# Two-layer graph attention: the second layer in steps of four key tiles, with logits in three pairs of banks and the mask applied in SBUF

## The chip, the cores and the metric

The kernel runs on one core of a Trainium2 chip. The metric is the device time of one execution in microseconds (us); of several runs the median is given. A profile shows one such execution. Engines are called PE or TensorE (matmuls), DVE or VectorE, ACT or ScalarE, POOL or GpSimd, and SP, whose queue issues the DMAs.

## The reference

Two attention layers over a graph of 4096 nodes with 512 features, 8 heads of 64, each with layer norm and a residual.

```python
# layer 0 (additive attention); adj holds edge weights, about 0 or up to 1e9
h = relu(layernorm(x))
d = (h @ W.T + b).reshape(N, 8, 64)
e = leaky_relu(src(d)[h, n] + trg(d)[h, m], 0.01) + adj
x = x + softmax(e, over m) @ d
# layer 1 (dot-product attention, masked)
h = relu(layernorm(x))
q, k, v = h @ Wq[head], h @ Wk[head], h @ Wv[head]
a = q @ k.T / 8 - 1e16 * (1 - max(adj, eye))
x = x + concat(softmax(a, over keys) @ v) @ Wo
```

All in float32.

## The kernel before

The program works through three stages. A preparation makes the first layer's values and logit parts and goes through the rows of `adj` in sets. The first layer runs over 8 query blocks of 512 queries by 32 key tiles of 128 keys; in the same loop it turns the rest of `adj` into a byte mask for the second layer, written to DRAM as `m_d`. It ends each query block by `finish` (normalise, residual, layer norm) and `project`, a generator whose matmuls are taken up in small portions by `fill(n)`, and which writes keys, queries and values of the second layer to `k_d`, `q_d`, `v_d`. `step_endings()` moves every unfinished generator of `endings` one `yield` on. The order of all instructions is the order in which the Python program issues them (a manual schedule); each engine works through its own queue in that order and waits for semaphores where data or buffers need it.

The change is in the second layer. Its work is 8 query blocks x 4 head pairs = 32 rounds, counted by `j`; a round has 32 key tiles of 128 keys, for two heads and 512 queries. Before, a step `s` covers two key tiles, so a round has `ST` = 16 steps and there are 512 steps. A step issues:

- `scores(s)` (L684): for each of two tiles four matmuls of 64x64x512, for the two heads and two halves of the tile, into a pair of PSUM banks, tag `q0` or `q1` (a pair holds 128x1024 f32: keys on partitions, heads and queries along the row).
- `exps` (L690): ScalarE's exponential of each tile, in place in PSUM.
- `masked` (L698): VectorE multiplies the exponentials in PSUM by the byte mask `mk` in SBUF and writes the product to `ring`, a buffer of 16 rows of 512 that holds 8 tiles (`share(t)`).
- `paired` (L703): GpSimd adds the two tiles of the step into `adds` (in a round's first step into `sums`).
- `gained(s - 1)` (L708): VectorE adds the last step's `adds` to `sums`, which becomes the denominators.
- `attended(s - 2)` (L716): four matmuls of values by `ring`, accumulated into `ot` over a round, in bank `m0` or `m1`.
- `fill` (project or output matmuls, L442) and `step_endings`.

The matmuls of `attended` lag two steps behind the logits, so that exponentials and masks of a step have time while TensorE works on others. At a round's end `divide(j)` copies `ot` to `both`, sums `sums` over partitions by a matmul with ones (`sp`, L730), sends the result through DRAM (`dd_d`, L734; `den`, L737) into a layout in which VectorE can take reciprocals (`rc`, L740), sends these through DRAM again (`rb`, L745) and lets GpSimd scale the output (L747). After four rounds `output` (L442, L759) applies `Wo`. Keys, values and queries of the next round (`load_keys`, `load_values`, `load_queries`) and masks of the next block (`load_mask`, two buffers of 2 MB) are loaded ahead by SP.

PSUM has eight banks: `q0` and `q1` (two each), `m0`, `m1`, `m2`, `s`. In the first layer `m0` and `m1` also serve `values` and `project`; in the second `project` uses `m1` and `m2`.

Of the kernel before, what the change touches and what calls it, by code (L numbers as in the profile page):

```python
# [8 lines left out]
F32 = mybir.dt.float32  # L9
I32 = mybir.dt.int32  # L10
U8 = mybir.dt.uint8
AF = mybir.ActivationFunctionType
# [5 lines left out]
P = 128  # L18
# [12 lines left out]
def tile_fast(  # L31
# [69 lines left out]
    q_d = dram.tile([NK, HC, P, W], F32, name="q_d")  # L101
    k_d = dram.tile([HC, P, N], F32, name="k_d")
    v_d = dram.tile([HC, P, NT, P], F32, name="v_d")
    dd_d = dram.tile([NK, HC, 2, W], F32, name="dd_d")
    rd_d = dram.tile([NK, HC, 2, W], F32, name="rd_d")

    def rows_of(t, n):
# [8 lines left out]
            nc.sync.dma_start(rows_of(t, n)[a], of[bass.ts(a, SQ)])  # L116

    ring = big.tile([P, 16, W], F32, name="ring")
    l0 = ExitStack()
    ppen = l0.enter_context(tc.tile_pool(name="pen", bufs=2))  # L120
    pmu = l0.enter_context(tc.tile_pool(name="mu", bufs=2))
# [127 lines left out]
    def prepare(pre):  # L249
# [113 lines left out]
            nc.scalar.activation(th[:, tiles], t, AF.Exp, scale=SLOPE - 1.0)  # L363

        def values(g, n, tiles):
            vp = ps.tile([P, tiles, W], F32, tag=("m0", "m1", "q1")[n], name="vp")
            for i in range(tiles):
                for kc in range(KC):
                    nc.tensor.matmul(
                        vp[:, i], lhsT=hT2[:, g % 2, kc, bass.ts(n + i, P)], rhs=wt[:, kc],  # L370
                        start=(kc == 0), stop=(kc == KC - 1),
                    )
            return vp
# [72 lines left out]
            if next(e, e) is e:  # L446
                endings.remove(e)

    banks = ["m0", "m1"]
    weights = {}  # L450

    def project(k, h1T):

        at = [0]

        def bank():
            at[0] += 1
            return ps.tile([P, W], F32, tag=banks[at[0] % 2], name="mp")

        def across(w, c, to):  # L460
            mp = bank()
# [174 lines left out]
    l0.close()  # L636


    ST = NT // 2
    ppa = ctx.enter_context(tc.tile_pool(name="pa", bufs=1))  # L640
    pq = ctx.enter_context(tc.tile_pool(name="q", bufs=3))
    prb = ctx.enter_context(tc.tile_pool(name="rb", bufs=2))
    pss = ctx.enter_context(tc.tile_pool(name="ss", bufs=1))
    total = NK * HC * ST
    banks[:] = ["m1", "m2"]
    ks, vs, qs, ms_, oTs, scs = {}, {}, {}, {}, {}, {}
    adds = ppa.tile([P, 2, 2, W], F32, name="adds")
    sums = ppa.tile([P, 2, 2, W], F32, name="sums")
    b6 = big.tile([P, AR * QK], F32, tag="B6", name="b6")
    wot = b6[:, N:].rearrange("p (c o) -> p c o", c=HC)  # L650

    def load_keys(j, cols):
        if j < NK * HC:
# [15 lines left out]
            qs[j] = pq.tile([P, W], F32, name="qt")  # L669
            nc.sync.dma_start(qs[j], q_d[j // HC, j % HC])  # L670

    def load_mask(k):
        if k < NK:
            ms_[k] = big.tile([P, NH * W], I32, tag=("B2", "B4")[k % 2], name="mk")
            nc.sync.dma_start(ms_[k], m_d[k])

    def scores(s):
        j, n = divmod(s, ST)
        for i in range(2):
            sc = scs[2 * s + i] = ps.tile([P, 2, W], F32, tag=f"q{i}", name="sc")  # L680
            for half in range(2):
                for h in range(2):
                    rows = bass.ts(h, D)
                    nc.tensor.matmul(  # L684
                        sc[bass.ts(half, D), h], lhsT=ks[j][rows, bass.ds((2 * n + i) * P + half * D, D)],
                        rhs=qs[j][rows], start=True, stop=True,
                    )

    def exps(t):
        nc.scalar.activation(scs[t], scs[t], AF.Exp, bias=shift, scale=1.0 / D**0.5)  # L690

    def share(t):
        return ring[:, bass.ts(t % 8, 2)]

    def masked(t):
        n = t % NT
        m = ms_[t // (HC * NT)].bitcast(U8).rearrange("p (h i l) -> p h l i", h=NH, l=4)[:, n // 4, n % 4]
        nc.vector.tensor_tensor(share(t), scs.pop(t), m.unsqueeze(1).to_broadcast([P, 2, W]), ALU.mult)  # L698

    def paired(s):  # L700
        j, n = divmod(s, ST)
        to = sums[:, j % 2] if n == 0 else adds[:, s % 2]
        nc.gpsimd.tensor_add(to, share(2 * s), share(2 * s + 1))  # L703

    def gained(s):
        j, n = divmod(s, ST)
        if n > 0:
            nc.vector.tensor_add(sums[:, j % 2], sums[:, j % 2], adds[:, s % 2])  # L708

    def attended(s):  # L710
        j, n = divmod(s, ST)
        if n == 0:
            oTs[j] = ps.tile([P, W], F32, tag=f"m{j % 2}", name="ot")
        for i in range(2):
            for h in range(2):
                nc.tensor.matmul(  # L716
                    oTs[j][bass.ts(h, D)], lhsT=vs[j][:, 2 * n + i, bass.ts(h, D)],
                    rhs=share(2 * s + i)[:, h],
                    start=(n == 0 and i == 0), stop=(n == ST - 1 and i == 1),
                )  # L720

    def divide(j):
# [2 lines left out]
        to = outs[k][:, c]  # L725
        nc.scalar.copy(to, oTs.pop(j))
        yield
        sp = ps.tile([P, W], F32, tag="s", name="sp")
        for h in range(2):
            nc.tensor.matmul(sp[bass.ts(h, SQ)], lhsT=ones, rhs=sums[:, j % 2, h], start=True, stop=True)  # L730
        sS = pss.tile([P, W], F32, name="sS")
        nc.scalar.copy(sS[:D], sp[:D])
        for h in range(2):
            nc.sync.dma_start(dd_d[k, c, h : h + 1], sS[h * SQ : h * SQ + 1])  # L734
        yield
        d = den[:, j]
        nc.sync.dma_start(d, dd_d[k, c].rearrange("h (p i) -> p h i", i=4))  # L737
        yield
        rc = small.tile([P, 2, 4], F32, name="rc")
        nc.vector.reciprocal(rc, d)  # L740
        nc.sync.dma_start(rd_d[k, c].rearrange("h (p i) -> p h i", i=4), rc)
# [22 lines left out]
    with tc.manual_schedule():  # L764
        load_queries(0)
        early = (NK - 1) * W
        load_keys(0, slice(0, early))
        load_mask(0)
        load_values(0, slice(0, early // P))
        for s in range(total + 4):  # L770
            j, n = divmod(s, ST)
            if s == 13:
                load_keys(0, slice(early, N))
                load_values(0, slice(early // P, NT))
                load_queries(1)
                nc.sync.dma_start(wot, wo.rearrange("h d o -> (h d) o").rearrange("(c p) o -> p c o", p=P))
            if s == 15:
                load_keys(1, slice(0, N))
                load_values(1, slice(0, NT))
            if n == 2 and j > 0:  # L780
                load_keys(j + 1, slice(0, N))
            if n == 4 and j > 0:
                load_values(j + 1, slice(0, NT))
            if n == 8 and j > 0:
                load_queries(j + 1)
            if j % HC == 1 and n == 6:
                load_mask(j // HC + 1)
            if s < total:
                scores(s)
                for i in range(2):  # L790
                    exps(2 * s + i)
                for i in range(2):
                    masked(2 * s + i)
                paired(s)
            if 0 <= s - 1 < total:
                gained(s - 1)
            a = s - 2
            if 0 <= a < total:
                attended(a)
                if a == ST - 1:  # L800
                    both = big.tile([P, 2, KC, W], F32, tag="B3", name="both")
                    for i in range(NK):
                        outs[i] = both[:, i % 2]
            fill(4 if s < ST + 6 else 2 if n % 8 == 5 else 0)
            step_endings()
            if s < ST - 4:
                step_endings()
            if 0 <= a < total and a % ST == ST - 1:
                e = divide(a // ST)
                next(e)  # L810
                endings.append(e)
# [28 lines left out]
        tp = ps.tile([P, W], F32, tag="m1", name="okt")  # L840
        nc.tensor.transpose(tp[:1, :P], ok, ident)
        nc.vector.tensor_reduce(flag, tp[:1, :P], AX.X, ALU.min)

# [239 lines left out]
```

## Time and profile before

| | |
|---|---|
| runs | 4362.02, 4365.09, 4366.08 us; median 4365.09 us |
| the profiled execution, own time | 4363.34 us |
| its span, first to last instruction | 4361.5 us |
| mean granted TensorE clock | 0.983 |
| PE busy | 4147.6 us (95%) |
| DVE busy | 3767.8 us (86%) |
| ACT busy | 1577.6 us (36%) |
| POOL busy | 2118.4 us (49%) |
| DMA | 555.53 MB, mean 127 GB/s |

The second layer begins at about 2170 us and ends with the program. Busy time counts an instruction from its start to its end, also while it stands still for something. In the profile, `x480: 1212/1215/2120` behind a line means 480 instructions that took at least 1212, in the median 1215 and at most 2120 ns. In a timeline the first column is the start in us from the span's begin and the second the length, of one instruction or of a row of equal ones (`x2`); a bracket tells how long the engine had been idle and what it had waited for. Fp32 matmuls appear twice each in the counts.

### The profile page before, as it was taken

The numbers are of one execution on the slowest core, as the hardware profiler recorded it, in microseconds if no ns is written. First come the engines' busy times: TensorE is split into PE (matmuls) and PEld (weight loads), VectorE is DVE, ScalarE is ACT, GpSimd is POOL, SyncE is SP. The second block draws the span as 40 slices with busy tenths as digits, with TensorE's granted clock in tenths as the row PEclk, the third lists the DMA queues.
The fourth block names the chain that finished last, engine by engine and source line by source line (L and its number), as shares of the span: only waits on it lengthen the run. The fifth ranks groups of instructions, "written<-read, shape, count | busy, mean of one in ns | idle before, by whom it ended". The sixth has DMA issues, their size and how long they took to land.

```text
span 4361.5 us, 63046 instructions
## 1 busy us (share of the span) xinstructions
PE 4147.6 (95%) x23806; PEld 1133.3 (26%) x23806; DVE 3767.8 (86%) x4508; ACT 1577.6 (36%) x1830; POOL 2118.4 (49%) x1004
## 2 busy tenths in 40 slices
PE   6899899999989899999999999999999999999997
PEld 3422222222222222222222222222222222222222
DVE  5599999999999999977657888888888888888885
ACT  3311222222222222210135555555555555555553
POOL 3211212122221212203057888788778777788784
PEclk8999999999999999999999999999999999999999
DMA  7776566565566656543313222222213223222211
GB/s 196 223 191 181 172 169 181 161 195 166 164 178 180 188 154 181 157 125 90 133 59 142 77 84 95 87 83 93 107 65 110 88 68 107 88 89 86 88 59 33
DMA packets 384568, 555.53 MB, mean 127 GB/s; under 512 B 62016, under 2 KB 242496, under 8 KB 375040
## 3 DMA queue, kind: packets, MB, share of 16 engines
q1 hardware_dynamic: 384256, 551.42, 41.2%
q8 instruction: 189, 3.10, 0.3%
q14 instruction: 123, 1.01, 0.1%
HBM read 416.68 MB, written 134.61 MB: 126 GB/s over the span
## 4 chain that ended last, share of the span: by engine, by line
PE 49%; DVE 4%; POOL 1%; ACT 1%; DMA 1%; issue 0%; SPq 0%; DVEq 0%; POOLq 0%; ACTq 0%
PE sc L684 21%; PE ot L716 19%; PE o L572 2%; DVE ring L698 2%; PE op L442 2%; PE mp L442 2%; DVE sums L708 1%; PE s L579 1%; ACT sc L690 1%; PE sp L730 1%; POOL hn L531 1%; DMA mk<-m_d 0%; DMA xt<-x_d 0%; POOL adds L703 0%; SPq L116 0%
## 5 line engine op out<-in xcount | busy, mean ns | idle before, releaser
L703 POOL TENSOR_TENSOR adds<-ring 128x1024 f32<-128x1024 f32 x480 | 1521.4, 3170 | 440.3 <-DVE ring L698 440.3
L561 DVE SCALAR_TENSOR_TENSOR ring<-rk,th,ct 128x512 f32<-128x512 f32 x2048 | 1506.5, 802 | 68.7 <-PE s L579 56.4
L698 DVE TENSOR_TENSOR ring<-sc,mk 128x1024 f32<-128x1024 f32 x1024 | 1205.9, 1218 | 352.8 <-ACT sc L690 334.4
L690 ACT ACTIVATE sc<-sc,shift 128x1024 f32<-128x1024 f32 x1024 | 1073.8, 1084 | 896.0 <-PE sc L684 894.7
L572 PE MATMUL o<-ring,v0t 128*64 128x512 f32 x4096 | 1035.7, 613 | 46.2 <-DVE ring L561 37.0
L684 PE MATMUL sc<-qt,kt 64*64 64x512 f32 x8192 | 1028.8, 612 | 16.2 <-issue 8.7
L708 DVE TENSOR_TENSOR sums<-sums,adds 128x1024 f32<-128x1024 f32 x480 | 608.3, 1267 | 2.2 <-POOL adds L703 2.2
L716 PE MATMUL ot<-ring,b 128*64 128x512 f32 x2048 | 496.6, 606 | 0.0
L716 PE MATMUL ot<-ring,vt 128*64 128x512 f32 x2048 | 495.4, 605 | 0.0
L579 PE MATMUL s<-ring,et 128*2 128x512 f32 x4096 | 486.0, 592 | 0.0
L572 PEld LDWEIGHTS o<-ring,v0t 128*64 128x64 f32 x4096 | 305.3, 140 | 676.2 <-issue 357.1
L684 PEld LDWEIGHTS sc<-qt,kt 64*64 64x64 f32 x8192 | 227.6, 132 | 778.0 <-DVE ring L698 671.6
L154 POOL TENSOR_TENSOR parts<-nm,negown 128x8 f32<-128x8 f32 x64 | 12.8, 199 | 740.4 <-DVE nm L150 695.1
L173 POOL TENSOR_SCALAR mp<-mp 128x2 f32<-128x2 f32 x64 | 32.1, 502 | 586.7 <-DVE mp L172 534.0
L190 ACT ACTIVATE mu<-pen,mp 128x1024 uint8<-128x1024 f32 x128 | 184.6, 1442 | 319.5 <-DVE pen L184 319.3
L466 ACT COPY e<-mp 128x512 f32<-128x512 f32 x64 | 37.5, 586 | 650.7 <-PE mp L442 612.6
L442 PE MATMUL mp<-work,wb 128*64 128x512 f32 x1024 | 244.6, 603 | 0.0
L716 PEld LDWEIGHTS ot<-ring,b 128*64 128x64 f32 x2048 | 124.4, 136 | 357.0 <-issue 357.0
L716 PEld LDWEIGHTS ot<-ring,vt 128*64 128x64 f32 x2048 | 124.4, 136 | 353.5 <-issue 352.4
L188 ACT ACTIVATE adjs<-adjs,nmc 128x1024 f32<-128x1024 f32 x128 | 146.8, 1147 | 169.9 <-POOL pen L179 167.3
L203 DVE STREAM_TRANSPOSE stage<-adjs 128x1024 f32<-128x1024 f32 x128 | 158.3, 1236 | 27.0 <-DMA ct_d<-stage 25.9
L179 POOL TENSOR_SCALAR pen<-adjs 128x1024 f32<-128x1024 f32 x128 | 179.8, 1414 | 1.0 <-DMA adjs<-in_adj_dram 0.4
(116 smaller groups left out, 1823.2 us busy)
## 6 DMA issues: line engine op xcount, KB each, us to landing
adjs<-in_adj_dram SPq DMA_DIRECT2D x512, 128.0 KB
ct_d<-stage SPq DMA_DIRECT2D x32, 2048.0 KB
ct<-ct_d SPq DMA_DIRECT2D x256, 256.0 KB
v0t<-v_d SPq DMA_DIRECT2D x256, 256.0 KB
kt<-k_d SPq DMA_DIRECT2D x31, 2048.0 KB
vt<-v_d SPq DMA_DIRECT2D x16, 2048.0 KB
b<-v_d SPq DMA_DIRECT2D x15, 2048.0 KB
m_d<-mst SPq DMA_DIRECT2D x32, 512.0 KB
```

Of the source, the lines that this page charges most:

```text
L179: nc.gpsimd.tensor_scalar(S.pen, S.A, -1.0, BIG, ALU.add, ALU.mult)
L190: nc.scalar.activation(S.mu.rearrange("p (h c l) -> p h l c", c=SQ, l=4), S.pen.rearrange("p (h l c) -> p h l c", c=SQ, l=4), AF.Exp, bias ...
L442: nc.tensor.matmul(to[cols], lhsT=lhsT[:, cols], rhs=rhs, start=start, stop=stop)
L561: nc.vector.scalar_tensor_tensor(ring[:, s % 2 * H + h], rks[k][:, h], th[:, n, h : h + 1], cts[s], ALU.max, ALU.mult)
L572: nc.tensor.matmul(G.o[c // 2][bass.ts(h, D), c % 2], lhsT=v0s[s][:, bass.ts(2 * c + h, D)], rhs=ring[:, s % 2 * H + 2 * c + h], start=(n ...
L579: nc.tensor.matmul(G.s[bass.ds(j * SQ, 2)], lhsT=et[:, n, at, 1 - g : 3 - g], rhs=ring[:, s % 2 * H + at], start=(n == 0 and g == 0), stop ...
L684: nc.tensor.matmul(sc[bass.ts(half, D), h], lhsT=ks[j][rows, bass.ds((2 * n + i) * P + half * D, D)], rhs=qs[j][rows], start=True, stop=True,)
L690: nc.scalar.activation(scs[t], scs[t], AF.Exp, bias=shift, scale=1.0 / D**0.5)
L698: nc.vector.tensor_tensor(share(t), scs.pop(t), m.unsqueeze(1).to_broadcast([P, 2, W]), ALU.mult)
L703: nc.gpsimd.tensor_add(to, share(2 * s), share(2 * s + 1))
L708: nc.vector.tensor_add(sums[:, j % 2], sums[:, j % 2], adds[:, s % 2])
L716: nc.tensor.matmul(oTs[j][bass.ts(h, D)], lhsT=vs[j][:, 2 * n + i, bass.ts(h, D)], rhs=share(2 * s + i)[:, h], start=(n == 0 and i == 0), ...
```

## The change

A step now covers `GT` = 4 key tiles, so a round has `ST` = 8 steps and there are 256.

- Logits of tile `t` go to the pair of banks `q{t % 3}`: three pairs, six banks. The other two are `s` (now `ot`) and `m2` (now `sp`, `op`, and `project` in the second layer). The first layer's `values` and `project` use the two banks of a tile `spare` with the tag `q2`.
- The exponential writes straight to `ring`. The mask is applied in `ring` in place, by one VectorE instruction for two tiles (2048 elements a row), both heads by broadcast.
- GpSimd still adds tile pairs, two additions per step, into the halves of a buffer of 2048; `gained` adds 2048 per step. `sums` and `adds` lie in `acc`, of which there is one in round 0 and two later.
- `attended` lags one step instead of two, and has eight matmuls.
- `sp` is four matmuls (two heads, two halves), `dd_d` four stores; a new VectorE addition of the halves (`d4`) stands before the reciprocal.
- There is one mask buffer, loaded in eight pieces, each as soon as its part of the old mask is no longer needed.
- In round 0 the projection runs in larger portions (`fill(8)` twice a step), and the keys and values of the last four tiles, those of round 1 and `wot` are all loaded at the start of step 7.

The diff, without the purely mechanical parts:

```diff
-            vp = ps.tile([P, tiles, W], F32, tag=("m0", "m1", "q1")[n], name="vp")
+            vp = spare[:, n : n + 1] if n < 2 else ps.tile([P, tiles, W], F32, tag="q1", name="vp")
...
-            return ps.tile([P, W], F32, tag=banks[at[0] % 2], name="mp")
+            return banks[at[0] % 2] if banks else ps.tile([P, W], F32, tag="m2", name="mp")
...
-    ST = NT // 2
+    GT = 4
+    ST = NT // GT
...
+    def scores(t):
+        j, n = divmod(t, NT)
+        sc = scs[t] = ps.tile([P, 2, W], F32, tag=f"q{t % 3}", name="sc")
...
-    def exps(t):
-        nc.scalar.activation(scs[t], scs[t], AF.Exp, bias=shift, scale=1.0 / D**0.5)
+    def share(t, n=1):
+        return ring[:, bass.ds(t % 8 * 2, 2 * n)]
+
+    def exps(t):
+        nc.scalar.activation(share(t), scs.pop(t), AF.Exp, bias=shift, scale=1.0 / D**0.5)
...
-        nc.vector.tensor_tensor(share(t), scs.pop(t), m.unsqueeze(1).to_broadcast([P, 2, W]), ALU.mult)
+    def masked(s, i):
+        m = mk.bitcast(U8).rearrange("p h (i l) -> p h l i", l=4)[:, s % ST, bass.ds(2 * i, 2)]
+        two = share(GT * s + 2 * i, 2).rearrange("p (l h) i -> p l h i", h=2)
+        nc.vector.tensor_tensor(two, two, m.unsqueeze(2).to_broadcast([P, 2, 2, W]), ALU.mult)
...
-        nc.gpsimd.tensor_add(to, share(2 * s), share(2 * s + 1))
+        t = GT * s + 2 * i
+        to = sums(j) if n == 0 else adds(s)
+        nc.gpsimd.tensor_add(to[:, i], share(t), share(t + 1))
...
-            nc.vector.tensor_add(sums[:, j % 2], sums[:, j % 2], adds[:, s % 2])
+            nc.vector.tensor_add(sums(j), sums(j), more)
...
-            oTs[j] = ps.tile([P, W], F32, tag=f"m{j % 2}", name="ot")
+            oTs[j] = ps.tile([P, W], F32, tag="s", name="ot")
...
+        d4 = small.tile([P, 2, 2, 4], F32, name="d4")
+        nc.sync.dma_start(
+            d4.rearrange("p h l i -> p (h l) i"), dd_d[k, c].rearrange("h (p i) -> p h i", i=4)
+        )
+        yield
         d = den[:, j]
-        nc.sync.dma_start(d, dd_d[k, c].rearrange("h (p i) -> p h i", i=4))
-        yield
+        nc.vector.tensor_add(d, d4[:, :, 0], d4[:, :, 1])
...
+            if 0 < s < ST:
+                gained(s - 1, more.pop(s - 1))
             if s < total:
-                scores(s)
-                for i in range(2):
-                    exps(2 * s + i)
-                for i in range(2):
-                    masked(2 * s + i)
-                paired(s)
...
+                for i in range(GT):
+                    scores(GT * s + i)
+                    exps(GT * s + i)
+                    if i % 2:
+                        masked(s, i // 2)
+                        more[s] = paired(s, i // 2)
...
-            a = s - 2
+            a = s - 1
             if 0 <= a < total:
+                if s >= ST:
+                    gained(a, more.pop(a))
                 attended(a)
...
-            fill(4 if s < ST + 6 else 2 if n % 8 == 5 else 0)
+            fill(8 if first else 4 if n == 5 else 0)
```

More of the change, by code (lines that the diff above doesn't have):

```diff
@@ L103, in tile_fast @@
     v_d = dram.tile([HC, P, NT, P], F32, name="v_d")
-    dd_d = dram.tile([NK, HC, 2, W], F32, name="dd_d")
+    dd_d = dram.tile([NK, HC, 4, W], F32, name="dd_d")
     rd_d = dram.tile([NK, HC, 2, W], F32, name="rd_d")
@@ L118, in tile_fast @@
     ring = big.tile([P, 16, W], F32, name="ring")
+    spare = ps.tile([P, 2, W], F32, tag="q2", name="spare")
     l0 = ExitStack()
@@ L447, in step_endings @@
                 endings.remove(e)
-    banks = ["m0", "m1"]
+    banks = [spare[:, 0], spare[:, 1]]
     weights = {}
@@ L644, in tile_fast @@
     total = NK * HC * ST
[L645 to L648, printed above, removed]
+    banks.clear()
+    ks, vs, qs, oTs, scs, acc = {}, {}, {}, {}, {}, {}
+    acc[0] = ppa.tile([P, 2, 2, 2, W], F32, name="acc0")
     b6 = big.tile([P, AR * QK], F32, tag="B6", name="b6")
     wot = b6[:, N:].rearrange("p (c o) -> p c o", c=HC)
+    mk = big.tile([P, NH, W], I32, tag="B2", name="mk")
     def load_keys(j, cols):
@@ L670, in load_queries, with load_mask @@
             nc.sync.dma_start(qs[j], q_d[j // HC, j % HC])
-    def load_mask(k):
+    def load_mask(k, at):
         if k < NK:
-            ms_[k] = big.tile([P, NH * W], I32, tag=("B2", "B4")[k % 2], name="mk")
-            nc.sync.dma_start(ms_[k], m_d[k])
-    def scores(s):
-        j, n = divmod(s, ST)
-        for i in range(2):
[L680 to L687, printed above, removed]
@@ L689, in exps @@
-    def exps(t):
[L690 to L703, printed above, removed]
@@ L705, in gained @@
-    def gained(s):
+            nc.sync.dma_start(mk[:, at], m_d[k].rearrange("p (h i) -> p h i", h=NH)[:, at])
+    def scores(t):
+        j, n = divmod(t, NT)
+        sc = scs[t] = ps.tile([P, 2, W], F32, tag=f"q{t % 3}", name="sc")
+        for half in range(2):
+            for h in range(2):
+                rows = bass.ts(h, D)
+                nc.tensor.matmul(
+                    sc[bass.ts(half, D), h], lhsT=ks[j][rows, bass.ds(n * P + half * D, D)],
+                    rhs=qs[j][rows], start=True, stop=True,
+                )
@@ new lines, in share, with sums @@
+    def share(t, n=1):
[6 more added lines that the diff above has]
+        nc.vector.tensor_tensor(two, two, m.unsqueeze(2).to_broadcast([P, 2, 2, W]), ALU.mult)
+    def sums(j):
+        return acc[j % 2][:, 0]
@@ L706, in gained, with adds, paired @@
+    def adds(s):
+        return acc[s % 2 if len(acc) > 1 else 0][:, 1]
+    def paired(s, i):
+        j, n = divmod(s, ST)
+        t = GT * s + 2 * i
+        to = sums(j) if n == 0 else adds(s)
+        nc.gpsimd.tensor_add(to[:, i], share(t), share(t + 1))
+        return to
+    def gained(s, more):
         j, n = divmod(s, ST)
         if n > 0:
-            nc.vector.tensor_add(sums[:, j % 2], sums[:, j % 2], adds[:, s % 2])
+            nc.vector.tensor_add(sums(j), sums(j), more)
     def attended(s):
@@ L712, in attended @@
         if n == 0:
-            oTs[j] = ps.tile([P, W], F32, tag=f"m{j % 2}", name="ot")
-        for i in range(2):
+            oTs[j] = ps.tile([P, W], F32, tag="s", name="ot")
+        for i in range(GT):
             for h in range(2):
                 nc.tensor.matmul(
-                    oTs[j][bass.ts(h, D)], lhsT=vs[j][:, 2 * n + i, bass.ts(h, D)],
-                    rhs=share(2 * s + i)[:, h],
-                    start=(n == 0 and i == 0), stop=(n == ST - 1 and i == 1),
+                    oTs[j][bass.ts(h, D)], lhsT=vs[j][:, GT * n + i, bass.ts(h, D)],
+                    rhs=share(GT * s + i)[:, h],
+                    start=(n == 0 and i == 0), stop=(n == ST - 1 and i == GT - 1),
                 )
@@ L727, in divide @@
         yield
-        sp = ps.tile([P, W], F32, tag="s", name="sp")
+        yield
+        sp = ps.tile([P, W], F32, tag="m2", name="sp")
         for h in range(2):
-            nc.tensor.matmul(sp[bass.ts(h, SQ)], lhsT=ones, rhs=sums[:, j % 2, h], start=True, stop=True)
+            for i in range(2):
+                nc.tensor.matmul(
+                    sp[bass.ts(2 * h + i, SQ)], lhsT=ones, rhs=sums(j)[:, i, h], start=True, stop=True
+                )
         sS = pss.tile([P, W], F32, name="sS")
-        nc.scalar.copy(sS[:D], sp[:D])
-        for h in range(2):
-            nc.sync.dma_start(dd_d[k, c, h : h + 1], sS[h * SQ : h * SQ + 1])
+        nc.scalar.copy(sS, sp)
+        for i in range(4):
+            nc.sync.dma_start(dd_d[k, c, i : i + 1], sS[i * SQ : i * SQ + 1])
+        yield
+        d4 = small.tile([P, 2, 2, 4], F32, name="d4")
+        nc.sync.dma_start(
+            d4.rearrange("p h l i -> p (h l) i"), dd_d[k, c].rearrange("h (p i) -> p h i", i=4)
+        )
         yield
         d = den[:, j]
-        nc.sync.dma_start(d, dd_d[k, c].rearrange("h (p i) -> p h i", i=4))
-        yield
+        nc.vector.tensor_add(d, d4[:, :, 0], d4[:, :, 1])
         rc = small.tile([P, 2, 4], F32, name="rc")
@@ L767, in tile_fast @@
         load_keys(0, slice(0, early))
-        load_mask(0)
+        for n in range(NH):
+            load_mask(0, n)
         load_values(0, slice(0, early // P))
-        for s in range(total + 4):
+        more = {}
+        for s in range(total + 2):
             j, n = divmod(s, ST)
-            if s == 13:
+            first = s < ST
+            if s == ST:
+                assert not fills and not endings
+                both = big.tile([P, 2, KC, W], F32, tag="B3", name="both")
+                for i in range(NK):
+                    outs[i] = both[:, i % 2]
+                acc[1] = big.tile([P, 2, 2, 2, W], F32, tag="B4", name="acc1")
+            if s == ST - 1:
                 load_keys(0, slice(early, N))
@@ L776, in tile_fast @@
                 nc.sync.dma_start(wot, wo.rearrange("h d o -> (h d) o").rearrange("(c p) o -> p c o", p=P))
-            if s == 15:
                 load_keys(1, slice(0, N))
                 load_values(1, slice(0, NT))
+            if n == 1 and j > 0:
+                load_keys(j + 1, slice(0, N))
             if n == 2 and j > 0:
-                load_keys(j + 1, slice(0, N))
+                load_values(j + 1, slice(0, NT))
             if n == 4 and j > 0:
-                load_values(j + 1, slice(0, NT))
-            if n == 8 and j > 0:
                 load_queries(j + 1)
-            if j % HC == 1 and n == 6:
-                load_mask(j // HC + 1)
-            if s < total:
-                scores(s)
-                for i in range(2):
-                    exps(2 * s + i)
-                for i in range(2):
-                    masked(2 * s + i)
-                paired(s)
-            if 0 <= s - 1 < total:
-                gained(s - 1)
-            a = s - 2
+            if j % HC == HC - 1 and n > 0:
+                load_mask(j // HC + 1, n - 1)
+            if j % HC == 0 and j > 0 and n == 0:
+                load_mask(j // HC, NH - 1)
+            if 0 < s < ST:
+                gained(s - 1, more.pop(s - 1))
+            if s < total:
+                for i in range(GT):
+                    scores(GT * s + i)
[3 more added lines that the diff above has]
+                        more[s] = paired(s, i // 2)
+            step_endings()
+            if first:
+                step_endings()
+                fill(8)
+            a = s - 1
             if 0 <= a < total:
+                if s >= ST:
+                    gained(a, more.pop(a))
                 attended(a)
[L800 to L803, printed above, removed]
-            fill(4 if s < ST + 6 else 2 if n % 8 == 5 else 0)
+            fill(8 if first else 4 if n == 5 else 0)
             step_endings()
-            if s < ST - 4:
+            if first:
                 step_endings()
@@ L839, in tile_fast @@
         nc.vector.tensor_reduce(ok, oks, AX.X, ALU.min)
-        tp = ps.tile([P, W], F32, tag="m1", name="okt")
+        tp = ps.tile([P, W], F32, tag="s", name="okt")
         nc.tensor.transpose(tp[:1, :P], ok, ident)
```

## The prediction

> **What bounds the kernel now.** I read the page first (engine busy shares, slices, the chain that ended last), then single lines, then timelines of two engines side by side. The chain says that the second layer is a chain of TensorE: L684 (logits) and L716 (values) hold 40% of the span, and waits for VectorE 4%.
>
> ```profile
> PE 49%; DVE 4%; POOL 1%; ACT 1%; DMA 1%; issue 0%; SPq 0%; DVEq 0%; POOLq 0%; ACTq 0%
> PE sc L684 21%; PE ot L716 19%; PE o L572 2%; DVE ring L698 2%; PE op L442 2%; PE mp L442 2%; DVE sums L708 1%; PE s L579 1%; ACT sc L690 1%; PE sp L730 1%; POOL hn L531 1%; DMA mk<-m_d 0%; DMA xt<-x_d 0%; POOL adds L703 0%; SPq L116 0%
> ```
>
> One head pair with one query block (a "round", 32 key tiles, 16 steps) is the repeating unit. Between the first POOL add (`sums`) of two neighbouring rounds lie 65.30 us, and in that stretch TensorE is never idle, VectorE is busy 56.2 us, GpSimd 52.1 us:
>
> ```profile
> 3535.47:3600.77 65.30, 65.15 (x412) 16.09 (x408) 56.17 (x50) 34.70 (x34) 52.13 (x18) 1.00 0.24 82
> ```
>
> The columns are the window, its length, then busy time and count on PE, weight loads, DVE, ACT and POOL, then granted clock, DMA share and GB/s. So the question is what each engine's round becomes. The decisive view is the durations by line, minimum, median and maximum in ns:
>
> ```profile
> L703 POOL TENSOR_TENSOR adds<-ring x480: 2348/3217/3374, 2188.0 to 4315.7; 128x1024 f32<-128x1024 f32 x160
> L703 POOL TENSOR_TENSOR sums<-ring x32: 2350/3284/3284, 2180.8 to 4253.9; 128x1024 f32<-128x1024 f32 x32
> L708 DVE TENSOR_TENSOR sums<-sums,adds x480: 1212/1215/2120, 2195.0 to 4318.6; 128x1024 f32<-128x1024 f32 x160
> L698 DVE TENSOR_TENSOR ring<-sc,mk x1024: 1191/1215/1226, 2178.4 to 4314.0; 128x1024 f32<-128x1024 f32 x171
> ```
>
> The same POOL add costs 2.35 us or 3.2 us. L708 is usually 1.21 us, but up to 2.12. L698, which reads its logits from PSUM, never varies. The timeline gives the reason:
>
> ```profile
> 3564.06 1.26 POOL L747 TENSOR_TENSOR both<-both,rb 128x512 f32<-128x512 f32 x1
> 3564.39 2.02 DVE L708 TENSOR_TENSOR sums<-sums,adds 128x1024 f32<-128x1024 f32 x1
> 3565.29 3.34 POOL L703 TENSOR_TENSOR adds<-ring 128x1024 f32<-128x1024 f32 x1
> 3566.33 2.34 DVE L698 TENSOR_TENSOR ring<-sc,mk 128x1024 f32<-128x1024 f32 x2
> ...
> 3602.08 2.36 DVE L698 TENSOR_TENSOR ring<-sc,mk 128x1024 f32<-128x1024 f32 x2 [0.26 <-ACT sc L690]
> 3604.58 2.36 POOL L703 TENSOR_TENSOR adds<-ring 128x1024 f32<-128x1024 f32 x1 [0.53 <-DVE ring L698]
> ```
>
> L708 has two SBUF inputs. It starts while POOL's L747 runs, gets nothing done until that ends (3565.32), then needs its usual 1.21 us (to 3566.41). L703, started at 3565.29, in turn ends 2.22 us after L708's end: it stood still until then. The add at 3604.58 meets only L698, from PSUM, and takes 2.36 us. So a VectorE operation with two SBUF inputs and a GpSimd operation exclude each other for whole instructions; each handover hides about 0.12 us. The first layer shows how hard this is: L561 (two SBUF inputs, back to back) keeps an operation that takes 0.77 us elsewhere waiting for 23 us.
>
> ```profile
> 1989.27 24.60 DVE L561 SCALAR_TENSOR_TENSOR ring<-rk,th,ct 128x512 f32<-128x512 f32 x37
> 1991.09 23.43 POOL L531 TENSOR_SCALAR hn<-wx,rstd,off 128x512 f32<-128x512 f32 x1 [6.25 <-PE htp L536]
> ```
>
> **The change, part by part.** *TensorE.* Per step of two tiles it starts logits at 3000.78, values at 3002.66, logits again at 3004.53: 1.88 us per group. A tile's worth of matmuls inside a group costs 0.857 us: L716 x8 takes 1.94 us, three groups run together (x24, at 4312.59) 5.37 us, (5.37 - 1.94)/4. A step is then 4 x 0.857 = 3.43 us plus 0.36 us for two switches between logits and values, 3.79 us. After: 8 x 0.857 + 0.36 = 7.22 us per four tiles instead of 7.58. This is the gain offered: 0.36 x 8 = 2.9 us per round.
>
> *ScalarE.* It writes to SBUF instead of PSUM: 1.09 us per tile at L690, 1.01 us for a copy of the same shape from PSUM to SBUF (L495); 4.3 us per four tiles, below all else. The bank is free after the exponential instead of after the mask, and with three pairs the logits never wait for VectorE directly.
>
> *VectorE.* Two masks and one sum per four tiles, each 2048 elements wide. From 0.68 us for 512 (L759) to 1.215 for 1024 (L708) one element costs 1.045 ns, so 2048 take 2.28 us. Three make 6.85 us, against 2 x (2 x 1.215 + 1.215) = 7.29 now. Taken alone it fits under 7.22.
>
> *GpSimd.* The adds stay as they are, two of 128x1024 per four tiles, 2.35 us free of conflict.
>
> *What the change adds.* The mask now reads ring and mask, both in SBUF. No row of this trace has one SBUF input in f32 and one in bytes, so I bound it: as L698 (one SBUF input: no conflict) or as L708 (two: full exclusion). It is nearest to L708, since what tells L698 from L708 is that one operand lies in PSUM, and this is what the change removes; L698's byte mask shows only that a byte operand alone does no harm. I take L708. The Trainium skill, "SBUF — State Buffer", section "Who interferes with whom", speaks against the change: a VectorE instruction with two SBUF inputs contends with a GpSimd instruction that reads SBUF, whole instruction against whole instruction; it makes no exception for byte operands, which no row here can show. Without the hidden handovers, as the page has it, a step would be 11.55 us and the total about 5190 us.
>
> With exclusion, each four tiles need, one after the other, 3 x 2.28 + 2 x 2.35 = 11.54 us, less five handovers of 0.12, or 10.94 us. No order escapes that: the sum waits for the adds, the adds for the masks, and the ring holds only two steps, so neither engine can run ahead for long. A round: 8 x 10.94, less the sum that its first step lacks (2.16), plus `both*rb` (1.14), is 86.5 us. If POOL's adds run in pairs behind two masks (the starvation above), the pair hides 0.08 less (2.30 us from add to add at 2180.79 and 2183.09, against 2.22) and the sum, woken by the second add, starts 0.03 after it instead of 0.12 before: up to 0.3 us per step, 88.9 us. I take 87.5. TensorE's 7.22 us per step, ScalarE, and the output matmuls (four yields at n=5, 3.4 us) all lie under this.
>
> Now: rounds 1 to 30 take 4253.87 - 2299.28 = 1954.6 us and the last 61.8 to its last add, together 2016.4. After: 31 x 87.5 = 2712.5. **+696 us** (86.5: +665; 88.9: +739).
>
> *Round 0* is 118.5 us (first `sums` add 2180.79 to 2299.28). TensorE after: 8 x 7.22 = 58; the projection's 48 yields x 0.857 = 41; transposes of `finish` about 8; twelve waits for the one projection bank (copy 0.59 plus about 0.2) = 10; the last keys are now loaded in the step that reads them (256 KB, about 4 us), and the next round's keys queue behind 1.75 MB (2 MB took some 10 us at 2486: about 8 us more than now). Together 129 us, with the locked 8 x 10.94 = 88 us beneath. **+10 us**, from -8 to +22.
>
> *Divide.* `sp` is 4 matmuls side by side instead of 2, same length. The new VectorE add waits for d4: behind it queue that step's successors, the masks of n=3, and after them values and exponentials. Unloaded, `sp` to reciprocal takes 5 us (4320.00 to 4324.95); behind the 2 MB of values, issued just before, about 14. VectorE comes to it only at the end of step n=2, one locked step (10.9 us) plus 5 to 8 us after `sp`: zero. Without that cover, 5 us per round, 155 in all. *Mask loading* in eight pieces has a whole round's lead: zero. *Tail:* two adds and a wide sum instead of one and a narrow one after the last mask, +3; two steps less to drain, -3: zero, within 5.
>
> Sum against the profiled execution (span 4361.5, own time 4363.34): 4363.3 + 696 + 10 = 5069.3. It lay 1.75 us below the median, so 5071; I say **5070**.
>
> **Rivals.** *A, faster: a byte operand doesn't count as the second SBUF input.* Then masks run free, only the sum excludes POOL (2 x 2.35 + 2.16 = 6.9 us, just under 7.22), and TensorE sets the end: -2.9 x 31 = -90, +10 for round 0: 4285 us, between 4260 and 4320. For it: L698 reads the same bytes beside POOL without a trace of conflict. Against: there they are the only SBUF operand. It decides as soon as adds beside masks stay at 2.35 us. *B, slower still: the divide's chain loses its cover.* If d4 lands more than about 16 us after `sp`, VectorE stands still with both POOL adds already done, and 5 to 10 us per round come on top: 5225 to 5380. For it: d4 is a gather of 16-byte pieces, queued behind 2 MB. Against: `den` lands before its reader in every round now, with 2 MB issued right behind it. *C: the change does nothing measurable*, if what TensorE gains were just given back. It would need exclusion to cost 3 us of a round, where the rows give 22.
>
> **How the numbers follow.** Exclusion as computed 0.85, A 0.09, B 0.05, C 0.01. The likeliest case runs from 86.5 us per round with a cheap round 0 (5020) to 88.9 with a dear one (5130). A byte mask could be 5% off the f32 row either way (16 x 0.12 x 31 = 60): 4980 to 5190, and I reach to 5200 for the weaker half of B. A is left out. A measurement of this kernel tells about 0.2% (9 us) from no change: faster 0.09, same 0.01, slower 0.90.
>
> **What would show it.** Right: adds of POOL at 4.4 us and more instead of 3.2, hardly any at 2.35; masks or sums stretched past 2.3 us; VectorE and GpSimd busy (waiting included) near 100% in the second layer; TensorE's idle time before the values ended by VectorE; rounds of 86 to 89 us. Wrong: adds at 2.35 beside masks, TensorE still without gaps and rounds of 62 us (A); VectorE idle before `den` by several us in each round (B).

## The result, and the profile after

The changed kernel takes 5055.82 us in the median of four runs (5053.20 to 5062.35), against 4364.32 us before (four runs): a ratio of 1.159, 95% interval 1.157 to 1.161. The forecast was 5070. The profiled execution is the longest of the four: 5062.35 us, with a span of 5060.5, 699.0 us more than before.

The chain that ended last, by engine and by line, has gone over to VectorE:

```profile
DVE 51%; PE 28%; issue 16%; DMA 2%; POOL 1%; SPq 1%; ACT 1%; DVEq 0%; ACTq 0%; POOLq 0%
DVE ring L698 20%; DVE acc L716 18%; PE o L573 12%; DVE ring L562 9%; PE s L580 6%; PE spare L443 5%; DVE den L754 1%; DVE nm L151 1%; PE mp L443 1%; PE spare L370 1%; DVE stage L204 1%; DMA m_d<-mst 1%; PE vp L370 1%; SPq L112 1%; POOL hn L532 1%
```

The windows view over thirty rounds (window, length, busy time and count on PE, weight loads, DVE, ACT and POOL, granted clock, DMA share, GB/s) shows VectorE busy all the time and TensorE idle for a fifth:

```profile
2330.00:4927.00 2597.00, 2065.87 (x12192) 579.88 (x12188) 2595.96 (x777) 1046.79 (x1022) 2177.59 (x510) 0.93 0.19 66
```

The durations by line (minimum, median, maximum in ns) tell why. The lines are POOL's pair adds, the mask in place, VectorE's sums in their two forms, and the new 8-element addition of the divide:

```profile
L710 POOL TENSOR_TENSOR acc<-ring x512: 2341/4398/4432, 2192.3 to 5007.1; 128x1024 f32<-128x1024 f32 x171
L698 DVE TENSOR_TENSOR ring<-ring,mk x512: 2240/3362/4460, 2190.0 to 5002.6; 128x2048 f32<-128x2048 f32 x171
L716 DVE TENSOR_TENSOR acc<-acc x116: 2258/4438/4451, 2217.4 to 5011.5; 128x2048 f32<-128x2048 f32 x116
L716 DVE TENSOR_TENSOR acc<-acc,acc x108: 4428/4439/4455, 2362.6 to 5004.8; 128x2048 f32<-128x2048 f32 x108
L754 DVE TENSOR_TENSOR den<-d x32: 169/2310/2321, 2355.8 to 5020.4; 128x8 f32<-128x8 f32 x32
```

The minima are close to what the prediction gave the operation alone: 2.24 us for a mask and 2.26 for a sum of 2048 elements, 2.34 for an add (the second form of the sum never runs alone). The maxima are the sum of two operations: 2.24 + 2.2 for a mask, 2.34 + 2.1 for an add. Even the 8-element addition takes 2.31 us where it has to let a POOL add go by, which is so in 31 of its 32 cases. The timeline shows the queue:

```profile
3498.11 8.76 POOL L710 TENSOR_TENSOR acc<-ring 128x1024 f32<-128x1024 f32 x2
3500.23 4.44 DVE L716 TENSOR_TENSOR acc<-acc,acc 128x2048 f32<-128x2048 f32 x1
3504.59 6.64 DVE L698 TENSOR_TENSOR ring<-ring,mk 128x2048 f32<-128x2048 f32 x2
3509.16 4.28 POOL L710 TENSOR_TENSOR acc<-ring 128x1024 f32<-128x1024 f32 x1 [2.29 <-DVE ring L698]
3511.14 4.44 DVE L716 TENSOR_TENSOR acc<-acc 128x2048 f32<-128x2048 f32 x1
```

The order of ends is add, sum, add, mask, mask, add: 3502.52, 3504.66, 3506.87, 3509.02, 3511.22, 3513.44. Each operation ends 2.14 to 2.22 us after the one before it, whichever engine runs it, and five make a step of 10.92 us. What the busy figures of the two engines count as work is, nearly half of the time, standing still: the two are busy for 2596.0 + 2177.6 us in a stretch of 2597 us in which one at a time gets on.

### The profile page after: what moved, and what is told of

Its sections match the earlier page's. It is cut to its first block, busy times and chain, and to the rows that moved or that the text cites. A ratio compares the mean times of both kernels' runs of the same rounds, so it can differ in the third digit from the quotient of the medians.

```text
span 5060.5 us, 62461 instructions
## 1 busy us (share of the span) xinstructions
PE 4277.4 (85%) x23934; PEld 1239.3 (24%) x23934; DVE 4714.5 (93%) x3772; ACT 1580.7 (31%) x1830; POOL 2762.6 (55%) x1004
## 4 chain that ended last, share of the span: by engine, by line
DVE 51%; PE 28%; issue 16%; DMA 2%; POOL 1%; SPq 1%; ACT 1%; DVEq 0%; ACTq 0%; POOLq 0%
DVE ring L698 20%; DVE acc L716 18%; PE o L573 12%; DVE ring L562 9%; PE s L580 6%; PE spare L443 5%; DVE den L754 1%; DVE nm L151 1%; PE mp L443 1%; PE spare L370 1%; DVE stage L204 1%; DMA m_d<-mst 1%; PE vp L370 1%; SPq L112 1%; POOL hn L532 1%
## 5 line engine op out<-in xcount | busy, mean ns | idle before, releaser
L710 POOL TENSOR_TENSOR acc<-ring 128x1024 f32<-128x1024 f32 x512 | 2200.8, 4321 | 560.5 <-DVE ring L698 560.5
L698 DVE TENSOR_TENSOR ring<-ring,mk 128x2048 f32<-128x2048 f32 x512 | 1701.1, 3366 | 60.7 <-ACT ring L693 60.7
L693 ACT ACTIVATE ring<-sc,shift 128x1024 f32<-128x1024 f32 x1024 | 1076.7, 1112 | 1242.3 <-PE sc L684 965.6
L684 PE MATMUL sc<-qt,kt 64*64 64x512 f32 x8192 | 947.4, 600 | 6.6 <-issue 6.3
L724 PE MATMUL ot<-ring,vt 128*64 128x512 f32 x2048 | 571.2, 695 | 261.5 <-DVE ring L698 259.8
L724 PE MATMUL ot<-ring,b 128*64 128x512 f32 x2048 | 569.6, 694 | 241.5 <-DVE ring L698 239.9
L716 DVE TENSOR_TENSOR acc<-acc 128x2048 f32<-128x2048 f32 x116 | 499.9, 4309 | 27.1 <-POOL acc L710 27.1
L716 DVE TENSOR_TENSOR acc<-acc,acc 128x2048 f32<-128x2048 f32 x108 | 479.4, 4439 | 0.0
L684 PEld LDWEIGHTS sc<-qt,kt 64*64 64x64 f32 x8192 | 288.8, 133 | 655.5 <-issue 509.4
L443 PE MATMUL spare<-work,wb 128*64 128x512 f32 x896 | 217.0, 605 | 4.4 <-ACT e L467 3.6
```

The costliest lines, as they stand in the source:

```text
L443: nc.tensor.matmul(to[cols], lhsT=lhsT[:, cols], rhs=rhs, start=start, stop=stop)
L684: nc.tensor.matmul(sc[bass.ts(half, D), h], lhsT=ks[j][rows, bass.ds(n * P + half * D, D)], rhs=qs[j][rows], start=True, stop=True,)
L693: nc.scalar.activation(share(t), scs.pop(t), AF.Exp, bias=shift, scale=1.0 / D**0.5)
L698: nc.vector.tensor_tensor(two, two, m.unsqueeze(2).to_broadcast([P, 2, 2, W]), ALU.mult)
L710: nc.gpsimd.tensor_add(to[:, i], share(t), share(t + 1))
L716: nc.vector.tensor_add(sums(j), sums(j), more)
```

## The experiments

Rounds are counted here from the first logits of one to those of the next, in the median after the first few. The times of e1 to e4 are of one run each, beside a run of the kernel before of 4360.91 us; those of e5 to e7 are medians of several runs.

**e1: the mask from PSUM again, all else as changed.**

```diff
-        nc.scalar.activation(share(t), scs.pop(t), AF.Exp, ...)
+        nc.scalar.activation(scs[t], scs[t], AF.Exp, ...)
...
-        nc.vector.tensor_tensor(two, two, m.unsqueeze(2).to_broadcast([P, 2, 2, W]), ALU.mult)
+        for l in range(2 * i, 2 * i + 2):   # t, m: of one tile
+            nc.vector.tensor_tensor(share(t), scs.pop(t), m.unsqueeze(1).to_broadcast([P, 2, W]), ALU.mult)
```

> The changed kernel with one part undone: exponentials stay in PSUM and two VectorE masks per tile pair read them there, one SBUF input each (the byte mask). Steps of four, three pairs of banks, one mask buffer stay. Theory (two SBUF inputs of VectorE and GpSimd's reads exclude each other): masks 1.21 us again and never stretched, GpSimd's adds 2.35 to 4.5 us (only the sums stop them), TensorE the bound again. But a bank is now free only after the mask: the fourth tile of a step waits about 1 us (0.95 + 1.09 + 1.22 + 0.1 against 3 x 0.857), so about 8.2 us per step, 70 to 71 us per round, some 4560 us. Rival (the new step order, the single mask buffer or the bank rotation cost the time, not the SBUF mask): rounds stay at 86 us, about 5050 us.

4573.72 us, 70.93 us per round. The lines are the mask, POOL's adds and TensorE's logits. Behind the bars of the logits' line stand the busy time, the mean ns of one, and TensorE's own idle time ahead of it with what ended most of that:

```profile
L700 DVE TENSOR_TENSOR ring<-sc,mk x1024: 1171/1216/1226, 2187.8 to 4519.0; 128x1024 f32<-128x1024 f32 x171
L712 POOL TENSOR_TENSOR acc<-ring x512: 2347/2376/4407, 2190.8 to 4520.4; 128x1024 f32<-128x1024 f32 x171
...
L684 PE MATMUL sc<-qt,kt 64*64 64x512 f32 x8192 | 1003.0, 605 | 240.4 <-DVE ring L700 234.0
```

The logits in the kernel before:

```profile
L684 PE MATMUL sc<-qt,kt 64*64 64x512 f32 x8192 | 1028.8, 612 | 16.2 <-issue 8.7
```

Masks are never stretched, and the adds' median falls from 4.40 to 2.38 us. 482 us of the loss are gone with this one edit. What remains is for the most part the other thing expected: logits waiting for a bank until its mask is done. This keeps TensorE idle 254 times for 0.92 us, 234.0 us over the run (3.2 us in the kernel before).

**e2: half of each add.** The denominators of 256 of 512 queries are left out; two memsets outside the steps fill their places with ones.

```diff
-        nc.gpsimd.tensor_add(to[:, i], share(t), share(t + 1))
+        some = slice(0, W // 2)
+        nc.gpsimd.tensor_add(to[:, i, :, some], share(t)[:, :, some], share(t + 1)[:, :, some])
```

> The changed kernel with GpSimd adding only the first 256 of 512 queries (the other denominators are left out). Theory: VectorE's three wide instructions and GpSimd's two adds (1.26 us each as for 512 elements at L763) follow one another: 3 x 2.28 + 2 x 1.26 - 5 x 0.12 = 8.76 us per step, about 69 us per round, 4510 us; masks between 2.28 and 3.4 us. Rival (a wide mask in place with a byte operand is slow by itself, 3.4 us in the mean): VectorE stays at 2 x 3.4 + 2.3 = 9 us or more per step with masks at 3.4 whatever the adds, 73 us or more per round.

4513.82 us, 69.27 us per round. Halving GpSimd's own work shortens VectorE's round: the masks' maximum falls from 4.46 to 3.38 us, while their minimum stays.

```profile
L699 DVE TENSOR_TENSOR ring<-ring,mk x512: 2239/2765/3377, 2187.5 to 4457.7; 128x2048 f32<-128x2048 f32 x171
```

So it is not the shape, the byte operand or the writing in place that makes a mask slow; it is the length of what GpSimd does beside it.

**e3: the kernel before, with this part alone.**

```diff
-        nc.scalar.activation(scs[t], scs[t], AF.Exp, ...)
+        nc.scalar.activation(share(t), scs.pop(t), AF.Exp, ...)
...
-        nc.vector.tensor_tensor(share(t), scs.pop(t), m.unsqueeze(1).to_broadcast([P, 2, W]), ALU.mult)
+        nc.vector.tensor_tensor(share(t), share(t), m.unsqueeze(1).to_broadcast([P, 2, W]), ALU.mult)
```

> The kernel before with this one part of the change: the exponential goes to the ring and the mask is applied there in place, 1024 elements at a time; steps of two and all else as before. Theory: per step 2 x 1.215 + 1.215 + 2.35 us one after another, less about 0.4 of hidden handovers, 5.6 us; 16 of them give 89 us per round and about 5110 us: this part alone makes the whole loss, and somewhat more of it, as the handovers come twice as often. Rival (steps of four or the rest of the change cause the loss): about 4364 us or less, since banks are free earlier.

5109.96 us, 89.0 us per round. In place, the 1024-element mask that always took 1.2 us takes up to 3.4:

```profile
L698 DVE TENSOR_TENSOR ring<-ring,mk x1024: 1191/2291/3393, 2180.7 to 5058.9; 128x1024 f32<-128x1024 f32 x171
```

Steps of four, three pairs of banks and one mask buffer are not needed for the loss; on top of the mask in the ring they take some 50 us off it.

**e4: GpSimd writes but doesn't read.** Constants stand for the pair sums.

```diff
-        nc.gpsimd.tensor_add(to[:, i], share(t), share(t + 1))
+        nc.gpsimd.memset(to[:, i], 1.0)
```

> The changed kernel with each GpSimd add replaced by a memset of the same output (its denominators are constants): GpSimd writes to SBUF but reads nothing. If only GpSimd's reads exclude a VectorE instruction with two SBUF inputs (the Trainium skill, SBUF - State Buffer, section Who interferes with whom, says so; no run here has shown it): masks 2.28 us throughout, TensorE bound at 7.22 us per step, 62 us per round, about 4290 us; this is also the time that the change would have without the exclusion. If any use of SBUF by GpSimd excludes: masks are stretched by the memset's length, and the round lies between 62 and 80 us depending on it.

4269.71 us, 61.86 us per round.

```profile
L698 DVE TENSOR_TENSOR ring<-ring,mk x512: 2239/2285/3376, 2186.3 to 4215.8; 128x2048 f32<-128x2048 f32 x171
L710 POOL MEMSET acc<- x512: 941/952/959, 2169.0 to 4214.1; 128x1024 f32 x171
```

512 memsets in a stream of masks and sums, and none is delayed by more than 0.02 us, though 415 of them stand beside a mask for more than half of their length. (Only 31 masks take more than 2.30 us, and each of them stands beside `both*rb`, which still reads.) The rule of the Trainium skill ("SBUF — State Buffer", "Who interferes with whom"), that a write-only GpSimd operation doesn't contend, is thereby shown here. The run also gives an estimate of the price of the exclusion: 5055.82 - 4269.71 = 786 us. Without it the change would have been about 2% faster than the kernel before (4269.71 against 4360.91 us), if the adds' wait for the masks, which the memsets don't have either, costs nothing.

**e5 and e6: a version drawn from this.** To make TensorE switch less often (11 steps per round instead of 16) without a second SBUF input, a step should be as long as the banks allow without waiting for its own masks: three tiles. e6 differs from e5 in the first layer alone: `values` and `project` get two tiles of a pool of their own instead of two halves of one tile (the third pair of banks moves to another pool with that).

```diff
-    ST = NT // 2
+    GT = 3
+    ST = -(-NT // GT)      # ten steps of three tiles, one of two
...
-            sc = scs[2 * s + i] = ps.tile([P, 2, W], F32, tag=f"q{i}", name="sc")
+        sc = scs[t] = ps.tile([P, 2, W], F32, tag=f"q{t % 3}", name="sc")
...
+                for t in tiles_of(s):
+                    scores(t)
+                    exps(t)             # in PSUM
+                for t in tiles_of(s):
+                    masked(t)           # PSUM to ring
+                    if t % 2:
+                        paired(t // 2)
+                        if t > 1:
+                            gained(t // 2 - 1)
...
+            fill(4 if first or n == 5 else 0)
# e6, the projection in the first layer
-            return banks[at[0] % 2] ...          # banks = [spare[:, 0], spare[:, 1]]
+            return ps0.tile([P, W], F32, tag=banks[at[0] % 2], name="mp") ...   # banks = ["m0", "m1"]
```

> A version drawn from the theory: steps of three key tiles (ten of three and one of two per round), exponentials in place in PSUM and masked from there by VectorE with one SBUF input each, logits through three pairs of banks, so that a step's burst never waits for its own masks; sums by pairs as before, two mask buffers; the first layer's projection in the two halves of one tile, as in the changed kernel. Theory: masks 1.21 us, never stretched; TensorE the bound with 32 x 2 x 0.857 + 11 x 0.36 + 4.1 (sp and output) = 62.9 us per round against 65.3 before, 59 in the three rounds without output matmuls: 77 us less over 31 rounds, 8 us more at the first layer's end: about 4296 us. Rival (VectorE, busy 93% of such a step, gives the gain back by masks that come late for the values): 65 us per round, 4365 us or more.

> The last version, with the first layer's two projection banks as two tiles of a pool of their own instead of two halves of one tile, as in the kernel before. In the changed kernel nine steps of the first layer's last block take 8.94 us instead of 7.99, each with a projection group that waits for ScalarE's copy of the other half. Theory (one tile, two halves: the write of one half waits for the read of the other): no such step, the first logits about 8 us earlier, and the time about 8 us below that of the steps of three with one tile (about 4288 us). Rival (the later start is the spread of executions): no difference beyond 2 or 3 us.

e5: 4368.95 us, a ratio of 1.0008 (0.9999 to 1.0017): the gain failed to come. Rounds took 63.7 us, near the 62.9 of theory, and the three without output 61.2 where theory had 59, but the first round of each block with output took 68.7 to 70.1. e6: 4360.90 us, 8.05 us below e5 (0.9993 of before, 0.9984 to 1.0002). In the profiled executions its first logits come only 3.1 us earlier than in e5 (2179.1 against 2182.2), as e6's execution was 4.1 us behind when the part in question began. In the changed kernel a projection group into one half of `spare` starts when ScalarE has copied the *other* half out; with two tiles the eight steps of 8.94 us are back at 7.99. The last 18 key tiles of the first layer take 143.6 us in all five kernels with the one tile (the changed one, e1, e2, e4, e5) and 136.0 us in all four with two (before, e3, e6, e7). The lines are the copy and the next group, in the changed kernel:

```profile
2036.26 0.59 ACT L467 COPY e<-spare 128x512 f32<-128x512 f32 x1 [15.22 <-PE spare L443]
2036.90 1.94 PE L443 MATMUL spare<-wx,work 128*64 128x512 f32 x8 [0.73 <-ACT e L467]
```

**e7: output two steps later.** In e6's long rounds the timeline shows the output matmuls waiting for a GpSimd product issued in the same step, behind an add:

```profile
2521.05 3.28 POOL L709 TENSOR_TENSOR adds<-ring 128x1024 f32<-128x1024 f32 x1 [0.18 <-DVE ring L704]
2524.28 1.26 POOL L753 TENSOR_TENSOR both<-both,rb 128x512 f32<-128x512 f32 x1
2525.60 1.29 PE L443 MATMUL op<-b,both 128*64 128x512 f32 x4 [3.32 <-POOL both L753]
2526.92 0.69 DVE L765 TENSOR_TENSOR xt<-xt,op 128x512 f32<-128x512 f32 x1 [4.80 <-PE op L443]
```

```diff
-            fill(4 if first or n == 5 else 0)
+            fill(4 if first or n == 7 else 0)
```

> The last version with the four output portions of a round in step 7 instead of step 5. In its trace the first round of each block lasts 68.9 us against 63.7 in the others, and there TensorE waits 3.3 us in step 5 for GpSimd's last both*rb, which was issued in that very step, with VectorE and then the logits waiting behind it. Theory: two steps later (11 us) the product is long there, all rounds with output last 63.7 us, and seven such rounds give 36 us: about 4325 us, 0.9% under the kernel before. Rival (the long rounds come from the mask load or the next block's transfers, which stand in the same round): no change from 4361 us.

4344.97 us, a ratio of 0.9952 (0.9939 to 0.9966): the best of the versions that compute everything, 0.5% under the kernel before, though not the 4325 forecast. The long rounds are gone, but every round with output now takes 64.63 us instead of 63.73: the output's step is 9.95 us long in step 7, 9.05 in step 5. The trace shows where the 0.9 us lie:

```profile
2520.17 1.27 POOL L753 TENSOR_TENSOR both<-both,rb 128x512 f32<-128x512 f32 x1
2520.25 2.28 DVE L714 TENSOR_TENSOR sums<-sums,adds 128x1024 f32<-128x1024 f32 x1
2522.45 2.34 DVE L704 TENSOR_TENSOR ring<-sc,mk 128x1024 f32<-128x1024 f32 x2
2523.72 1.09 PE L690 MATMUL sc<-qt,kt 64*64 64x512 f32 x8 [0.82 <-DVE ring L704]
```

In step 7 of each of the 31 rounds the last tile's logits wait 0.8 us for a mask (in e6, 4 rounds have this wait). Ahead of that mask VectorE's sum takes 2.28 us instead of 1.23, beside `both*rb`: the exclusion again, in a place where TensorE has no slack. No run moved `both*rb` to test this.

## Why the prediction was right, point by point

**The mechanism** held for the rounds, which make 661 of the 699 us. Exclusion was read from an f32 row (L708) and carried over to a mask with a byte operand, by the argument that the change removes the PSUM operand; the masks of 3.4 and 4.4 us and e3 confirm it, and rival A is out. The step came to 10.92 us against 10.94 worked out, the round to 86.58 (30 rounds, 2329.67 to 4927.17) against a lower bound of 86.5. Two small errors are hidden in the step: the five operations alone take 11.42 us by their minima, not 11.54, and the handovers hide 0.10 us each, not 0.12.

**The sum, term by term**, against the profiled span of 699.0 us more:

| term | predicted | measured |
|---|---|---|
| rounds 1 to 31 | +696 | 2677.4 - 2016.4 = +661.0 |
| round 0 | +10 | 137.3 - 118.5 = +18.8 |
| up to the first add of the second layer | none | 2192.3 - 2180.8 = +11.5 |
| from the last add's start to the end | 0, within 5 | 53.4 - 45.8 = +7.6 |

The total is 7 us off partly by luck, since two kinds of error nearly cancel. The rounds were over-sized by 35 us: 28 because I took 87.5 us, above the bound, for adds running in pairs behind two masks, which the trace does not show (a sum goes between them), and 7 because I counted the last round whole where its last add comes after 79.9 us. The other three terms were under-sized by 28 us in all. I gave the first layer no term: moving `values` and `project` from `m0` and `m1` to two halves of one tile looked like a change of names. The nine traces show 7.6 us for it (143.6 against 136.0); the rest lies ahead of that block, where e6 and e7, with the same first layer, are also 4.8 us apart.

In round 0 the total was 9 us too small, and its parts were wrong one by one. I had put 10 us for twelve waits for the one projection bank and 12 for keys that land late, with 4 us for 256 KB that no run shows. There were six such waits of 0.7 us, 4.3 in all, and one of 0.36 us for keys. What I left out is the wait for the first layer's end, of which I had counted the transposes alone: it shares GpSimd and VectorE with the adds and masks. TensorE stands idle for GpSimd's `hn` for 10.9 us where it was 2.8 before, and 24.1 us in all where it was 15.9 (from the first logits to those of round 1). What makes the rest of the 18.8, no run tells apart.

At the tail the last add and sum run one after the other: from the last mask's end (5004.91) to the sum's end 8.9 us, against 4.6 before, where I had 3 more. Of the 7.6 us in the table, this makes 2.5 (from the last add's start to the sum's end 6.7 us, against 4.2). The other 5.1 come after the sum's end (46.7 against 41.6 us). There the granted clock is 0.68 against 0.81 before, and one group of output matmuls takes 6.39 us, where the next one of the same size takes 3.65: a term that I had put at nothing.

**The divide** (rival B) kept its cover: VectorE stood idle before `den` once in the whole run, 6.6 us, in the tail. **TensorE's gain** is real where nothing else binds: e4's round of 61.86 us is 3.4 less than before, where I had 2.9, and its 4269.71 us lie within the range given for A, 15 below its value. **Rival C** would have needed an exclusion of 3 us per round; e4 against the changed kernel gives 24.7.

The signs named beforehand came true but for one: adds at 4.4 us (9 of 512 stay under 2.5), masks and sums past 2.3, VectorE at 100%, and TensorE standing idle before the values until a mask is done, 499.7 us (none before):

```profile
L724 PE MATMUL ot<-ring,vt 128*64 128x512 f32 x2048 | 571.2, 695 | 261.5 <-DVE ring L698 259.8
L724 PE MATMUL ot<-ring,b 128*64 128x512 f32 x2048 | 569.6, 694 | 241.5 <-DVE ring L698 239.9
```

In the kernel before:

```profile
L716 PE MATMUL ot<-ring,b 128*64 128x512 f32 x2048 | 496.6, 606 | 0.0
L716 PE MATMUL ot<-ring,vt 128*64 128x512 f32 x2048 | 495.4, 605 | 0.0
```

The sign that failed is GpSimd: I had expected it near 100% as well, and it is at 84% in the thirty rounds (2177.59 of 2597 us). Once a step it has no add to run until VectorE's mask is done, as the idle 2.29 us before the add at 3509.16 show.

## What to carry to other kernels

Before moving an operand from PSUM to SBUF to free a bank sooner, count the SBUF inputs of the VectorE instructions that will read it, and look for GpSimd work beside them: with two SBUF inputs, and a GpSimd instruction that reads SBUF, add up the two engines' instructions as if one engine ran them. The evidence may already lie in the trace as a large spread between minimum and median of one line; compare the slow cases with what runs on the other engine, and with a line that never varies. Give each bank that is filled and emptied in turn a tile of its own, since two halves of one tile waited for each other here.

## What the runs showed that I had not expected

A tiny VectorE instruction waits out a whole add like a long one: the 8-element addition (two SBUF inputs) took 2.31 us in 31 of 32 rounds, each time until the POOL add beside it had ended, where it needs 0.17.

The granted clock fell to 0.93 between 2400 and 4100 us of the changed kernel, although TensorE was busy for less of that time (1351.6 of 1700 us); e2 and e4 show 1.00 and e3, as slow as the changed kernel and with TensorE busy for 1318.6 us, 0.99. The traces show where the two slow kernels differ. The clock is either full or half here: half in 61 stretches of the changed kernel, 246 us together, and in nine of e3, 34 us. TensorE's idle time is much the same, 346 and 367 us, but in the changed kernel it comes in longer pieces: 60 of them last 2.8 to 3.5 us, while none in e3 is longer than 1.5. No run changed the length of these pieces alone, so that they lower the clock is a guess. In the rounds TensorE's work did not set the time, so there this cost little, if anything; in the tail it did.
